# The FFN of the first two token blocks computed together, each prepared pair of weight tiles used for both

## The chip, the cores and the metric

One core of a Trainium2 chip runs the kernel. The metric is device time in microseconds (us) of one execution. Engines are named as in the profile: PE (TensorE; its weight loads are PEld), DVE (VectorE), ACT (ScalarE), POOL (GpSimd) and SP (SyncE, which issues nearly all DMAs here). L74 means line 74 of the kernel before, unless the text says that a line is of the changed kernel.

## The reference, cut to what matters

`x` has 4 sequences of 1024 tokens with 512 channels. After a layer norm `xn`, an attention branch and a gated FFN branch are added to `x`:

```
xn  = layernorm(x)
h   = rmsnorm(xn) * qkv_norm_w
q, k, v = h @ ternary(qkv_w).T              # 16 heads of 32
# chunks of 128 tokens, with a state S carried from chunk to chunk:
o   = scale * (decayed causal (q k^T) v  +  decayed q S);  S = lam_T * S + decayed k^T v
att = rmsnorm(rmsnorm(o, norm_w), proj_norm_w) @ ternary(proj_w).T
ffn = (silu(xn @ w_gate.T) * (xn @ w_up.T)) @ w_down.T     # hidden size 2048
out = x + att + ffn
```

`ternary(w)` rounds a matrix to -1, 0 or 1 times its mean magnitude.

## The kernel before, in words

**Number format.** PE works on fp16. An f32 value is kept as a pair of fp16 tiles, `hi` (rounded, after a scaling by a power of two) and `lo` (the rest). A product of two such pairs takes three matmuls (hi·hi, hi·lo, lo·hi).

**Tiling.** The 4096 tokens are 8 blocks of 512. `ffn_up` (L681) takes one block and one of 16 hidden tiles `j` of 128: 12 matmuls of 128x512 for the gate and 12 for the up product, each into a PSUM bank `psf` (three banks, shared with `ffn_down`). ACT takes the silu (L693), DVE multiplies (L696), ACT and POOL split the result into the pair `ghl` (L699, L700). `ffn_down` (L704) multiplies `ghl` with the down weights `wd`, and DVE adds the sums to `acc` (L720), which holds `x` and goes out when all its parts are in. A block's FFN is 48 steps; a step is what lies between two `yield`s.

**Weight preparation.** The FFN weights come in f32. Two hidden tiles (gate, up and down parts of each) are a group; there are 8. `load_group` loads the six tiles (256 KB each), `group_sums` finds their magnitudes on DVE (L312) and ACT (L316), `group_scale` makes a common power of two with a small PE matmul with a matrix of ones, a few small DVE operations behind it (L326 to L335), and `group_conv` makes hi (ACT L352) and lo (DVE L354, or POOL L357 and L360), and stores the gate and up pair to DRAM (`gu_d`, L362). Block 0 uses the tiles as they come out of this: `ffn0` (L743) walks over the 8 groups, with the down product of one group during the up products of the next, so that `acc` of block 0 gets 8 FFN sums per 128 tokens. `stage` (L777) places the preparation in the steps of block 0: `LEAD` says how many steps ahead of a group's use (six steps a group) each part of it is recorded. Blocks 1 to 7 run `ffn` (L730), which reads the prepared pairs back (512 KB per tile) and adds two sums per 128 tokens.

**Layer norm.** `ln_stats` computes the statistics on DVE (L389, L390), the inverse root on POOL (L395, L396) and normalises on DVE (L402). Block 0 is transposed into `xT` by PE (`ln0`, L412). Later blocks (`ln`, L430) get hi from ACT (L436), lo from POOL (L437) and are transposed by DMA (L438), during the last steps of the block before. One `xT` tile holds 512 tokens, and every up matmul reads all 512.

**Attention.** It runs in halves of 256 tokens (`att_half`, L458), whose steps are interleaved with those of the FFN. The list `at` (L841) gives the step at which each half begins: 36, then every 22.4 steps. A half computes q and k (L470 to L495; four pieces, ACT L479 and DVE L480 split them into hi and lo), writes them to DRAM (`sd`, L484) and reads them back head by head (`qst`, `kst`, L487), and k is also transposed by DMA (`kn`, L492). Then come v, the scores (one PSUM bank `pss`, DVE L545, ACT L547, POOL L548), the state and the projection. `prep` and `prep_proj` prepare the ternary weights beside block 0.

**Order.** A scheduler decides the order of the instructions on DVE, ACT, POOL and SP when the kernel is built; each engine then runs its list in order. PE keeps the program's order (L74).

Of the kernel before, what the change touches and what calls it, by code (L numbers as in the profile page):

```python
# [28 lines left out]
def block_kernel(ctx, tc, x, qkv_w, qkv_nwT, proj_w, proj_nwT, proj_nw, norm_w, s, w_gu, w_down, out):  # L29
# [83 lines left out]
    pnw_bc = ct([P, C], F32, "pnw_bc")  # L113
    ones = pnw_bc[:, :P]
    V.memset(ones, 1.0)
    nwT = ct([P, CC], F32, "nwT")
# [47 lines left out]

    HOLD = {"qst": (4, 1), "kst": (4, 1), "qhl": (2, 1), "khl": (2, 1)}

# [116 lines left out]
    def raw_pair(g, kind):  # L283

        if kind == 2:
            return [t32(), t32()]
        if g == 0 and kind == 0:
            t = wt([P, 2, C], F32, "kn", 1)
            return [t[:, 0, :], t[:, 1, :], t]
        return [wt([P, C], F32, *(("ghl", 8) if g % 2 else ("xin", 4) if g else ("xn2", 2))) for _ in range(2)]  # L290

# [120 lines left out]
    def ln0():  # L412

        rs, xts = lnst.pop(0)
        xT = wt([P, 2, CC, HB], F16, "xT", 1)
        blk[0] = [xT, None, rs]
        low = []
        for k in range(4):
            pt = bank(ps_f if k == 3 else ps_a, (P, CC, P))
            for c in range(CC):  # L420
                T.transpose(pt[:, c, :], xts[k][:, c * P : (c + 1) * P], ident)
            hi, lo = (xT[:, n, :, k * P : (k + 1) * P] for n in range(2))
            A.activation(hi, pt, AF.Copy, scale=XS)
            low.append((lo, pt, XS, hi, ALU.mult, ALU.subtract))
        for k in range(4):
            if k == 2:
                yield
            V.scalar_tensor_tensor(*low[k])

    def ln(b):  # L430
        rs, xts = lnst.pop(b)
        xT = wt([P, 2, CC, HB], F16, "xT", 1)
        blk[b] = [xT, None, rs]
        for k in range(4):
            xn2 = wt([P, 2 * C], F16, "xn2", 2).rearrange("p (a c) -> p a c", a=2)
            A.copy(xn2[:, 0, :], xts[k])  # L436
            G.tensor_tensor(xn2[:, 1, :], xts[k], xn2[:, 0, :], ALU.subtract)  # L437
            SY.dma_start_transpose(  # L438
                xT[:, :, :, k * P : (k + 1) * P].rearrange("p a c t -> p (a c) t"),
                xn2.rearrange("p a c -> p (a c)"),  # L440
            )
            yield
# [15 lines left out]
    def att_half(b, half):  # L458
# [5 lines left out]
        kst = wt([P, 4, CC, UT], F16, "kst", 1)  # L464
        qhl = wt([P, 2, CC, UT], F16, "qhl", 1)
        khl = wt([P, 2, CC, UT], F16, "khl", 1)
        qhi, qlo = qhl[:, 0], qhl[:, 1]
        khi, klo = khl[:, 0], khl[:, 1]
        kn = wt([P, 2, CC, 2, P], F16, "kn", 1)
        for i in range(4):  # L470
            dhi, dlo = (qhi, qlo) if i < 2 else (khi, klo)
            pair = slice(2 * (i % 2), 2 * (i % 2) + 2)
            pq = bank(ps_a, (P, 2, UT))
            for n in range(2):
                w = slice((2 * i + n) * P, (2 * i + n + 1) * P)
                for c in range(CC):
                    T.matmul(pq[:, n, :], wqkT[:, c, w], hhi[:, c, :], start=(c == 0), stop=False)
                    T.matmul(pq[:, n, :], wqkT[:, c, w], hlo[:, c, :], start=False, stop=(c == CC - 1))
            A.activation(dhi[:, pair, :], pq, AF.Copy, scale=QS)  # L479
            V.scalar_tensor_tensor(dlo[:, pair, :], pq, QS, dhi[:, pair, :], ALU.mult, ALU.subtract)  # L480
            if i % 2 == 1:
                src, dst, sel = (qhl, qst, (0, 1, 0)) if i == 1 else (khl, kst, (0, 0, 1))
                sd = dram.tile([P, 2 * CC * UT], F16, tag=f"sd{i}", name=nm("sd"), bufs=2)
                SY.dma_start(sd, src.rearrange("p a c t -> p (a c t)"))  # L484
                sv = sd.rearrange("(h d) f -> d h f", d=D)
                for g in range(3):
                    SY.dma_start(  # L487
                        dst[D * g : D * g + D].rearrange("p h c t -> p h (c t)"),
                        sv[:, :, sel[g] * CC * UT : (sel[g] + 1) * CC * UT],
                    )  # L490
                if i == 3:
                    SY.dma_start_transpose(  # L492
                        kn.rearrange("p a c k q -> p (a c k) q"), khl.rearrange("p a c t -> p (a c t)")
                    )
            yield  # L495

        vs, vrs = [], []
        for k in range(2):
# [3 lines left out]
            for c in range(CC):  # L502
                T.matmul(pv, hhi[:, c, hs], wvT[:, c, :], start=(c == 0), stop=False)
                T.matmul(pv, hlo[:, c, hs], wvT[:, c, :], start=False, stop=(c == CC - 1))
            vhl = wt([P, 2 * C], F16, "vhl", 5).rearrange("p (h a d) -> p h a d", a=2, d=D)
            pvh = pv.rearrange("p (h d) -> p h d", d=D)
# [21 lines left out]
        for k in range(2):  # L528
            u = Chunk()
            u.kn, u.vr = kn[:, :, :, k, :], vrs[k]  # L530
            u.g = g0 + k
# [43 lines left out]
        def state(u):  # L575
            pkv = bank(ps_a, (P, CC, P))
            for c in range(CC):
                ch = slice(c * P, (c + 1) * P)
                kh, kl = u.kn[:, 0, c, :], u.kn[:, 1, c, :]
                vh, vl = (v[:, ch] for v in u.vr)  # L580
# [16 lines left out]
        def norms(u):  # L597
# [19 lines left out]
            if u.g < B * N // P - 2:  # L617
                on = wt([P, 2 * C], F16, "vhl", 5).rearrange("p (a c) -> p a c", a=2)
                A.copy(on[:, 0, :], u.o3)  # L619
                G.tensor_tensor(on[:, 1, :], u.o3, on[:, 0, :], ALU.subtract)  # L620
                oT = wt([P, 2 * C], F16, "vhl", 5).rearrange("p (a c t) -> p a c t", a=2, t=P)
                SY.dma_start_transpose(
                    oT.rearrange("p a c t -> p (a c) t"), on.rearrange("p a c -> p (a c)")
                )
                u.oh, u.ol = oT[:, 0], oT[:, 1]
# [99 lines left out]
    def load_acc(b):  # L725
        for k in range(4):
            acc[4 * b + k] = load_x(4 * b + k, "acc", 8)
            parts[4 * b + k] = 1 + (2 if b else NG)

# [12 lines left out]

    def ffn0():  # L743
        prev = None

        def down(ks):
            g, gts = prev
            for k in ks:
                for _ in ffn_down(0, k, range(2 * g, 2 * g + 2), gts, icg[:, g : g + 1]):
                    pass  # L750

        for g in range(NG):
            nxt = g + 1 < NG
            gts = []
            for r in range(2):
                j = 2 * g + r
                for n, _ in enumerate(ffn_up(0, j, gu0.pop(j), bsc0, gts, G)):
                    stage(6 * g + 3 * r + n)
                    yield
                if g == 0 and r == 0:  # L760
                    load_acc(0)
                stage(6 * g + 3 * r + 2)
                if prev is not None and nxt:
                    down((2 * r, 2 * r + 1))
                    yield
            if not nxt:
                down((0, 1))
                yield
                down((2, 3))
                yield  # L770
            prev = (g, gts)
        down((0, 1))
        yield
        down((2, 3))
        yield

    def stage(i):  # L777
# [8 lines left out]
        for lead, f in zip(LEAD, (load_group, group_sums, group_scale, conv0, conv1)):  # L786
            g, m = divmod(i + lead, 6)
            if m == 0 and 0 < g < NG:
# [8 lines left out]

    LEAD = (16, 8, 5, 4, 2)
    load_group(0)
# [6 lines left out]
    with after(gate):  # L806
        group_conv(0, 1, (0, 1))
        group_sums(0, (2,))
        load_group(1)
        for i in range(5 - max(LEAD), 0):  # L810
            if i == -4:
                norm_sums()
            stage(i)

    def prep():
        qw = load_rows(qkv_w, ("qst", "kst", "qhl", "khl"))
        SY.dma_start(nw_bc, norm_w.partition_broadcast(P))
        yield from prep_qkv_w(qw)

    def prep_proj():  # L820
        pw = [wt([P, C], F32, "acc", 8) for _ in range(4)]
        for r in range(4):
            SY.dma_start(pw[r], proj_w[r * P : (r + 1) * P, :])
        yield
        with after(lg):
# [19 lines left out]
    halves = []  # L845
    side, side2 = prep(), prep_proj()
    t = 0
    for b in range(NB):
        lns = iter(())
        for i, _ in enumerate(ffn(b) if b else ffn0()):  # L850
            for _ in range(int(0.8 * t) - int(0.8 * (t - 1))):
                next(side, 1)
            if t == 12 or 28 <= t < 34 or 36 <= t < 56 and t % 2:
                next(side2, 1)
            if t in mh:
# [7 lines left out]
            t += 1  # L863
            if t == 6 * NG - 6:
                SY.dma_start(pnw_bc, proj_nw.partition_broadcast(P))
            if b + 1 < NB:
                if i == TS - (22 if b else 15):
                    ln_stats(b + 1)
                if i == TS - (9 if b else 5):
                    lns = ln(b + 1)  # L870
                if i in ((TS - 8, TS - 7, TS - 5, TS - 4) if b else range(TS - 4, TS)):
                    next(lns, 1)
        for _ in lns:
            pass
        if b == 0:
            half_scales(0)
# [53 lines left out]
```

## Time and profile before

| | us |
|---|---|
| median of 3 runs | 1369.12 (1367.17 to 1370.31) |
| the profiled execution: its own time | 1368.61 |
| its span in the trace | 1366.7 |
| PE busy | 1322.6 (97%), 8514 matmuls |
| DVE, ACT, POOL busy | 719.9, 550.3, 619.6 |
| chain that ended last: PE, DVE, POOL, issue, DMA | 79%, 7%, 7%, 3%, 3% |
| DMA | 178.11 MB, 130 GB/s in the mean, 343 GB/s in the first of 40 slices |

A matmul of 128x512 is listed with 0.38 us, but matmuls overlap: twelve of them in a row start 2.59 us before the next twelve. "Idle" below is time in which no PE row lies; each gap hides about 0.16 us more, the overlap that it interrupts. The granted TensorE clock is 1.00 or 0.50 at any moment; a mean between them says how long it was at half.

### The profile page before, as it was taken

The numbers are of one execution on the slowest core, as the hardware profiler recorded it, in microseconds if no ns is written. First come the engines' busy times: TensorE is split into PE (matmuls) and PEld (weight loads), VectorE is DVE, ScalarE is ACT, GpSimd is POOL, SyncE is SP. The second block draws the span as 40 slices with busy tenths as digits, with TensorE's granted clock in tenths as the row PEclk, the third lists the DMA queues.
The fourth block names the chain that finished last, engine by engine and source line by source line (L and its number), as shares of the span: only waits on it lengthen the run. The fifth ranks groups of instructions, "written<-read, shape, count | busy, mean of one in ns | idle before, by whom it ended". The sixth has DMA issues, their size and how long they took to land.

```text
span 1366.7 us, 21760 instructions
## 1 busy us (share of the span) xinstructions
PE 1322.6 (97%) x8514; PEld 695.6 (51%) x8514; DVE 719.9 (53%) x1415; ACT 550.3 (40%) x1033; POOL 619.6 (45%) x603
## 2 busy tenths in 40 slices
PE   5998989999999999999999999999999999999998
PEld 2443445554555545455455545555555555565554
DVE  7897764445544354453644446453553445356444
ACT  6754443343433334333334243342424334244341
POOL 3657672444624254353634246342545245255451
PEclk9999999999999999999999999999999999999999
DMA  9833836146261554426363354626283444535420
GB/s 343 294 124 114 231 101 180 48 137 156 87 191 31 165 128 125 140 59 173 94 155 108 103 141 104 178 69 162 80 181 95 116 116 106 142 109 124 105 66 31
DMA packets 155974, 178.11 MB, mean 130 GB/s; under 512 B 101600, under 2 KB 101600, under 8 KB 155872
## 3 DMA queue, kind: packets, MB, share of 16 engines
q1 hardware_dynamic: 155728, 176.73, 47.0%
q8 instruction: 66, 1.08, 0.3%
q14 instruction: 36, 0.29, 0.1%
q10 hardware_dynamic: 144, 0.01, 0.0%
HBM read 119.55 MB, written 33.55 MB: 112 GB/s over the span
## 4 chain that ended last, share of the span: by engine, by line
PE 79%; DVE 7%; POOL 7%; issue 3%; DMA 3%; ACT 1%; SPq 0%; POOLq 0%; ACTq 0%; DVEq 0%
PE psf L74 58%; PE psa L74 19%; PE pss L74 2%; DMA xin<-in_x_dram 2%; DMA xT<-xn 1%; POOL t L548 1%; DVE acc L720 1%; POOL xn L437 1%; DVE t L696 1%; DVE gs L312 1%; POOL rs L396 1%; POOL wd L360 1%; DVE t L239 0%; POOL ghl L700 0%; POOL gu L360 0%
## 5 line engine op out<-in xcount | busy, mean ns | idle before, releaser
L74 PE MATMUL psf<-xT,gu 128*128 128x512 f16 x3072 | 703.4, 381 | 10.6 <-POOL gu L360 5.5
L74 PEld LDWEIGHTS <-gu 128*128 128x128 f16 x3072 | 294.7, 98 | 338.0 <-issue 10.1
L74 PE MATMUL psf<-wd,ghl 128*128 128x512 f16 x1536 | 352.3, 380 | 2.7 <-ACT t L693 1.1
L74 PEld LDWEIGHTS <-ghl 128*128 128x128 f16 x1536 | 146.9, 98 | 164.3 <-issue 3.3
L548 POOL TENSOR_TENSOR t<-t,t 128x512 f16<-128x512 f32 x128 | 149.5, 1168 | 164.2 <-ACT t L547 163.9
L700 POOL TENSOR_TENSOR ghl<-t,ghl 128x512 f16<-128x512 f32 x86 | 102.6, 1193 | 163.4 <-ACT ghl L699 150.2
L696 DVE SCALAR_TENSOR_TENSOR t<-psf,bsc,t 128x512 f32<-128x512 f32 x128 | 95.9, 749 | 121.2 <-PE psf L74 104.8
L699 ACT CAST ghl<-t 128x512 f16<-128x512 f32 x128 | 79.0, 617 | 176.1 <-DVE t L696 175.6
L545 DVE SCALAR_TENSOR_TENSOR t<-pss,rs,mask 128x512 f32<-128x512 f32 x128 | 95.3, 744 | 77.2 <-PE pss L74 74.7
L693 ACT ACTIVATE t<-psf,ug 128x512 f32<-128x512 f32 x128 | 87.5, 684 | 98.0 <-PE psf L74 96.6
L74 PE MATMUL psa<-h,wqkT 128*128 128x256 f16 x1024 | 122.2, 273 | 0.0
L519 POOL TENSOR_TENSOR t<-t,t 128x512 f16<-128x512 f32 x28 | 32.6, 1163 | 195.3 <-ACT t L518 195.3
L547 ACT CAST t<-t 128x512 f16<-128x512 f32 x128 | 79.1, 618 | 101.9 <-DVE t L545 96.3
L74 PEld LDWEIGHTS <-wqkT 128*128 128x128 f16 x1024 | 99.7, 98 | 23.4
L720 DVE SCALAR_TENSOR_TENSOR acc<-psf,c,acc 128x512 f32<-128x512 f32 x56 | 41.8, 747 | 63.0 <-PE psf L74 62.7
L74 PEld LDWEIGHTS <-t 128*128 128x128 f16 x1040 | 47.6, 97 | 35.0 <-POOL t L548 3.4
L74 PE MATMUL psa<-wvT,h 128*128 128x512 f16 x256 | 60.5, 379 | 0.0
L74 PE MATMUL pss<-qst,kst 96*128 96x128 f16 x512 | 49.2, 218 | 8.7 <-DVE t L545 6.5
L74 PE MATMUL psa<-wpT,vhl 128*128 128x512 f16 x240 | 56.7, 379 | 0.0
L620 POOL TENSOR_TENSOR vhl<-t,vhl 128x512 f16<-128x512 f32 x30 | 34.7, 1155 | 48.0 <-ACT vhl L619 48.0
L573 POOL TENSOR_TENSOR t<-t,t 128x512 f32<-128x512 f32 x28 | 36.1, 1288 | 44.1 <-DVE t L572 18.6
L508 DVE SCALAR_TENSOR_TENSOR vhl<-psa,rs,vhl 128x512 f16<-128x512 f32 x32 | 24.0, 749 | 56.2 <-ACT vhl L507 54.5
(188 smaller groups left out, 1340.8 us busy)
## 6 DMA issues: line engine op xcount, KB each, us to landing
gu<-gu_d SPq DMA_DIRECT2D x112, 512.0 KB, 3.6
qst<-sd SPq DMA_DIRECT2D x48, 256.0 KB, 4.8
kst<-sd SPq DMA_DIRECT2D x48, 256.0 KB, 4.7
xin<-in_x_dram SPq DMA_DIRECT2D x32, 256.0 KB, 3.0
acc<-in_x_dram SPq DMA_DIRECT2D x32, 256.0 KB, 2.8
gu_d<-gu SPq DMA_DIRECT2D x16, 512.0 KB, 4.1
sd<-qhl SPq DMA_DIRECT2D x16, 512.0 KB, 2.6
sd<-khl SPq DMA_DIRECT2D x16, 512.0 KB, 3.3
```

Of the source, the lines that this page charges most:

```text
L74: tc.keep_in_program_order(nc.tensor.matmul(*a, **k))
L519: G.tensor_tensor(vrl, vr, vrh, ALU.subtract)
L545: V.scalar_tensor_tensor(sm, pss, u.rk, mask[:, 4 * qd : 4 * qd + 4, :], ALU.mult, ALU.mult)
L547: A.copy(u.smh, sm)
L548: G.tensor_tensor(u.sml, sm, u.smh, ALU.subtract)
L573: G.tensor_tensor(u.o, u.o, oc, ALU.add)
L620: G.tensor_tensor(on[:, 1, :], u.o3, on[:, 0, :], ALU.subtract)
L693: pa = A.activation(sl, pm, AF.Silu, scale=ug[:, j // 2 : j // 2 + 1])
L696: pv = V.scalar_tensor_tensor(gf, pm, bs[:, j // 2 : j // 2 + 1], sl, ALU.mult, ALU.mult)
L699: A.copy(ghl[:, 0, :], gf)
L700: E.tensor_tensor(ghl[:, 1, :], gf, ghl[:, 0, :], ALU.subtract)
L720: V.scalar_tensor_tensor(acc[g], ps, c, acc[g], ALU.mult, ALU.add)
```

## The change

The first two blocks are computed in one loop of 96 steps, `ffn01`, in place of `ffn0` and of `ffn(1)`. Each group is prepared once, at half the rate per step, and its two tiles serve block 0 and block 1; each block's `acc` gets the sum of every group, so block 1 also gets 8 FFN sums per 128 tokens and reads no prepared pair back. In the first group the order is both tiles for block 0, then both for block 1. Block 1's layer norm moves from the end of block 0 to the start of the kernel, and the attention halves keep their step numbers.

Other edits: `xT` has two buffers instead of one, `vhl` four instead of five; q and k go to DRAM in four pieces of 256 KB through a tile `qk` with three buffers, and k is transposed in two pieces as they come; the matrix of ones is a broadcast column; `proj_w` is loaded into the tile `qst` once the qkv weights are done with it, and its preparation follows theirs in one sequence.

```diff
-        xT = wt([P, 2, CC, HB], F16, "xT", 1)
+        xT = wt([P, 2, CC, HB], F16, "xT", 2)
...
         for i in range(4):
-            dhi, dlo = (qhi, qlo) if i < 2 else (khi, klo)
+            p = i % 2
+            hl = wt([P, 2, 2, UT], F16, "qk", 3)
...
-            if i % 2 == 1:
-                SY.dma_start(sd, src.rearrange("p a c t -> p (a c t)"))
...
+            SY.dma_start(sd[:, :, p], hl.rearrange("p a c t -> p a (c t)"))
+            if i > 1:
+                SY.dma_start_transpose(
+                    kn[:, p].rearrange("p a c k q -> p (a c k) q"), hl.rearrange("p a c t -> p (a c t)")
+                )
...
-            parts[4 * b + k] = 1 + (2 if b else NG)
+            parts[4 * b + k] = 1 + (2 if b > 1 else NG)
...
-    def ffn0():
+    def ffn01():
...
+        def down(units):
+            g, gts = prev
+            for u in units:
+                b, k = divmod(u, 4)
+                for _ in ffn_down(b, k, range(2 * g, 2 * g + 2), gts[b], icg[:, g : g + 1]):
+                    pass
         for g in range(NG):
             nxt = g + 1 < NG
-            gts = []
-            for r in range(2):
-                j = 2 * g + r
-                for n, _ in enumerate(ffn_up(0, j, gu0.pop(j), bsc0, gts, G)):
-                    stage(6 * g + 3 * r + n)
+            gts = [], []
+            order = [(0, 0), (1, 0), (0, 1), (1, 1)] if g else [(0, 0), (0, 1), (1, 0), (1, 1)]
+            for m, (b, r) in enumerate(order):
+                for n, _ in enumerate(ffn_up(b, 2 * g + r, gu0[2 * g + r], bsc0, gts[b], G)):
+                    stage(12 * g + 3 * m + n)
                     yield
...
                 if prev is not None and nxt:
-                    down((2 * r, 2 * r + 1))
+                    down((2 * m, 2 * m + 1))
                     yield
...
-            g, m = divmod(i + lead, 6)
+            g, m = divmod(i + lead, 12)
...
-    LEAD = (16, 8, 5, 4, 2)
+    LEAD = (14, 10, 8, 7, 4)
...
     with after(gate):
         group_conv(0, 1, (0, 1))
         group_sums(0, (2,))
+        ln_stats(1, 1)
+        for _ in ln(1):
+            pass
         load_group(1)
-        for i in range(5 - max(LEAD), 0):
-            if i == -4:
-                norm_sums()
-            stage(i)
+        norm_sums()
...
-    for b in range(NB):
+    for b in range(1, NB):
         lns = iter(())
-        for i, _ in enumerate(ffn(b) if b else ffn0()):
+        n_steps = TS if b > 1 else 2 * TS
+        for i, _ in enumerate(ffn(b) if b > 1 else ffn01()):
```

## The prediction

> **What bounds the kernel now.** I read the engine totals and the slices of the page first, then the busy time by stretches, then PE's waits and its timeline where a stretch shows idle time.
>
> ```profile
> PE 1322.6 (97%) x8514; PEld 695.6 (51%) x8514; DVE 719.9 (53%) x1415; ACT 550.3 (40%) x1033; POOL 619.6 (45%) x603
> DMA  9833836146261554426363354626283444535420
> ```
>
> PE is busy 97% of the span, and the change leaves its matmuls as many and as large as they are. So the change can only move PE's idle time and the time at half clock. Busy time by stretches (columns: stretch, its length, PE, PEld, DVE, ACT, POOL busy, clock, DMA share, GB/s) says where those are:
>
> ```profile
> 0.00:34.00 34.00, 18.88 (x71) 9.46 (x72) 26.66 (x77) 22.04 (x49) 12.38 (x26) 0.95 0.94 343
> 34.00:100.00 66.00, 64.21 (x306) 30.02 (x305) 59.61 (x137) 44.11 (x94) 38.74 (x30) 1.00 0.61 209
> 100.00:131.00 31.00, 24.61 (x108) 10.80 (x107) 21.41 (x39) 15.80 (x33) 26.33 (x21) 0.89 0.36 122
> 131.00:177.00 46.00, 41.46 (x238) 22.02 (x237) 33.93 (x62) 19.55 (x34) 30.77 (x29) 1.00 0.75 201
> 177.00:335.00 158.00, 155.86 (x1023) 82.64 (x1021) 80.89 (x152) 61.22 (x111) 68.90 (x69) 1.00 0.48 130
> 335.00:515.00 180.00, 174.74 (x1175) 92.36 (x1174) 84.92 (x166) 65.05 (x121) 80.95 (x84) 1.00 0.42 115
> ```
>
> Idle in the five from 34 on: 1.8, 6.4, 4.5, 2.1, 5.3. The rows that own it, from PE's waits between 90 and 200 and from PE's timeline at the head and at 117 (start, length, what, idle before):
>
> ```profile
> PE psf L74 <- POOL gu L360: 5.5, 2, 5.0
> PE pss L74 <- DMA kst<-sd: 1.8, 1, 1.8
> PE psf L74 <- DMA xT<-xn: 1.2, 1, 1.2
> ...
> 26.68 0.87 PE L74 MATMUL psa<-gm,pnw_bc 128*128 128x3 f32 x4 [2.84 <-DVE gm L318]
> 27.41 9.30 PE L74 MATMUL psf<-xT,gu 128*128 128x512 f16 x36
> ...
> 125.26 4.26 PE L74 MATMUL psf<-xT,gu 128*128 128x512 f16 x10 [5.03 <-POOL gu L360]
> ```
>
> At 120 PE waits 5.03 us for POOL to finish a weight tile, then runs ten matmuls in 4.26 us where ten take 2.32: a wait of that size costs 1.9 us more at half clock. The 2.84 us wait at the head does the same (36 matmuls in 9.30, where they take 7.93).
>
> **What the change can take away.** Block 0's preparation, now in 48 steps beside the start of the attention, is spread over 96. In each group PE gets 31 us of FFN instead of 15.6, while POOL's four L360 and two L357 (4 x 1.2 + 2 x 1.7 = 8.2 us) stay the same. So the 5.03 us wait and its half clock should go. The wait for block 1's `xT` at 177 goes too, because its layer norm is no longer there. Waits of that kind and the bursts around them, 34 to 335: idle 1.8 + 6.4 + 4.5 + 2.1 = 14.8, half clock 1.9, and about twelve gaps that each hide 0.16 of overlap, 1.9. Sum 18.6 us.
>
> What stays of it? DVE gets 24 more adds (L720 at 0.747: 17.9 us) and the second half of the preparation while attention runs. I put it near 17 of 25 us from 43 to 344, twelve stretches of 25. The quiet stretch above (DVE 12.8 of 25) loses 2.1 in 158, which makes 4 over 300. Six stretches of the trace with DVE at 16 or more of 25 (at 75, 125, 500, 675, 825, 1225) lose 0.1, 0.3, 2.5, 2.2, 0.0 and 1.3, mean 1.07, which makes 12.8. The ones that lose little are those without a layer norm next to the scores, as this stretch will be, so I take 5 and keep 4 to 12.8. Gain 13.6.
>
> **What it costs at the head.** The built program's order of instructions shows that block 1's layer norm has to be finished before PE's fifth up product, the first for block 1. Rows for its price, from the groups kept apart by form, and from the DMA issues:
>
> ```profile
> L437 POOL TENSOR_TENSOR xn<-xin,xn 128x512 f16<-128x512 f32 x8 | 10.1, 1267 | 8.3 <-ACT xn L436 8.3
> L389 DVE BATCH_NORM_STATS2 st<-xin 128x6 f32<-128x512 f32 x16 | 11.0, 690 | 20.3 <-DMA xin<-in_x_dram 20.2
> L402 DVE TENSOR_SCALAR xin<-xin,mv,rs 128x512 f32<-128x512 f32 x15 | 10.1, 716 | 2.4 <-POOL rs L400 2.2
> ...
> xT<-xn SPq DMA_TRANSPOSE x28, 3.5
> kn<-khl SPq DMA_TRANSPOSE x16, 6.4
> ...
> nw_bc<-in_norm_w_dram SPq DMA_DIRECT2D x1, 256.0 KB, 11.5
> ```
>
> First matmul: two reductions of group 1 (L312, 0.675 each) and a small operation now stand on DVE ahead of group 0's scale, 1.5 us. A third stands ahead of its first lo part, 0.7. So 24 matmuls that ended at 23.7 end at 25.9. The wait that follows shrinks: before it was for group 1's sums, now only for the magnitude of group 0's down part, which DVE has at about 26.3. With 0.7 for the small matmul, PE goes on at 27.0 without half clock, and 24 more end at 32.2. Before they ended at 27.41 + 1.37 + 5.18 = 34.0.
>
> Then block 1's `xT`. From group 0's scale (17.2) to the last normalised tile DVE has 38 instructions: four lo parts 3.0, four reductions 2.7, four statistics 2.8, four aggregates 0.7, four normalisations 2.9, one L696 0.75, and some twenty small ones 3.0; sum 15.9, end 33.1. From 32.3 POOL still has a small product, three lo parts, one `ghl` and another small one: 0.3 + 3 x 1.27 + 1.26 + 0.4 = 5.8, end 38.1. Each transpose waits for its lo part, the last lands 3.5 later, at 41.6. PE idles 9.4 and then loses 1.9 at half clock: it is at its 49th up matmul 43.5 - 34.0 = 9.5 us later than before. Behind the transposes SP holds group 2's loads and two `gu_d` writes; group 2 is used 24 steps on, some 60 us, so they are covered. The wait also lets DVE, ACT and POOL catch up.
>
> [...] The trace has 1.27 (POOL L437) beside 0.75 to 0.88 on DVE (L354), so 1.4 to 1.7 times. [...] The sum goes by the row.
>
> **The rest.** No gu reads for block 1: 16 of 512 KB less, no PE wait names them, 0. The q and k pieces: 48 more SP issues of about 0.4 us, but k's transpose (L492, 3.3 to 4.8 us of SP) no longer stands whole before the kst reads; kst was waited for 1.8 us in all, counted above. Bounds for later blocks: from -5.3 (all idle of 335 to 515) to +1.8 (one such wait more); I take 0, since PE's order there is unchanged. Four `vhl` buffers: no wait for one shows; 0, upper bound one wait like the 2.84 with its 1.4. Ones as a broadcast and the later `proj_w`: 0: the matmuls with ones are a dozen of 0.2 to 0.4, and the preparation of `proj_w` is recorded up to about step 33, while `qst` is first overwritten near step 38 and the projection comes near 58; if it were late, the row for a wait on `qst` is 0.4.
>
> **Sum.** -18.6 + 5 + 9.5 = -4.1 against the profiled execution's own 1368.6 (span 1366.7, 1.9 around it): 1364.5. It lies 0.5 under the median of the runs, so 1365.0. About 0.2%, 2.7 us, is what a measurement here can tell from no change.
>
> **The rivals.**
> *Transposes held up (slower).* The place is the head: the first 50 us of the trace run DMA full (share 0.94), and transfers issued at 24 to 26 there took 11.5 us. If the last transpose takes that in place of 3.5, PE waits 8 longer: 1373. It decides from a landing of about 10.3 us on (3.5 and 4.1 + 2.7 more). Against: some 11.5 MB stand before the transposes, at 343 GB/s or more done by about 35, before the last is issued.
> *DVE limits the attention.* What stays is 12.8 in place of 5: 1372.8. For: 24 adds and the preparation fall beside scores that have one PSUM bank. Against: at 75 DVE is busy 24.75 of 25 and PE idles 0.1.
> *Later blocks gain.* kst earlier removes the idle of 335 to 515: 1359.7. For: the SP time of L492. Against: only 1.8 us of waits name kst.
>
> **How the numbers follow.** Forecast 0.47 (own range 1362 to 1370: DVE's rows start up to a tenth closer than their lengths, 1.6 less, and 0.9 less stays; upward 9 stays and POOL is 1 later); transposes 0.20; DVE 0.20; later blocks 0.13. Faster: 0.37 of the forecast and 0.13; same: 0.10, 0.02 of the transposes and 0.06 of DVE; slower: 0.18 and 0.14. Range: the third rival with the forecast's low end, 1357, to the first with 9 staying, 1377.
>
> **What would show it.** Right: a PE wait of 7 to 11 us for `xT` near 32 to 42, half clock behind it, no PE wait for POOL L360, under 8 us idle from 43 to 335. Wrong: no wait at the head or one over 15, PE waiting at `pss` for DVE all through the first 340 us, or idle that moves by more than 5 after 340.

## The result, and the profile after

| | kernel before | changed kernel |
|---|---|---|
| median, us | 1369.26 (1367.17 to 1370.31) | 1399.98 (1398.97 to 1401.95) |
| ratio | | 1.0228 (95% interval 1.0210 to 1.0246) |
| span of the profiled execution | 1366.7 | 1397.2 |

The change makes the kernel 2.3% slower, 30.5 us by the spans; the forecast was 4.1 us faster. From here on, line numbers of the changed kernel are some lines lower: L691 (was L696) multiplies silu and up product, L694 (was L699) makes the `hi` part of `ghl`, L403 (was L402) normalises, L438 and L439 (were L437 and L438) make a token tile's `lo` part and transpose it, L543 (was L548) makes the scores' `lo` part, L611 (was L616) ends the attention's norms, L715 (was L720) adds a sum to `acc`.

Engine totals of the page after, then the DMA slices:

```profile
PE 1329.7 (95%) x8514; PEld 697.5 (50%) x8514; DVE 734.2 (53%) x1433; ACT 549.4 (39%) x1033; POOL 625.8 (45%) x618
DMA  9332625237571562517454354624364353436430
```

The matmuls are as many as before. PE's busy time rose by 7.1, most of it by matmuls at half clock (PE was busy for 22.3 us at half clock, before for 10.8), and the other 23.4 of the 30.5 is new idle time. DVE has 14.3 more to do, by 18 instructions more in all. None of these sums says where it was lost. Busy time by stretches, with bounds shifted so that they hold about the same work as those of before (columns: stretch, length, PE, PEld, DVE, ACT, POOL, clock, DMA share, GB/s):

```profile
0.00:47.00 47.00, 22.24 (x81) 10.76 (x82) 34.56 (x88) 24.84 (x53) 27.22 (x49) 0.85 0.94 319
...
110.00:138.00 28.00, 25.51 (x123) 11.88 (x121) 20.04 (x39) 12.94 (x26) 16.21 (x13) 1.00 0.29 94
138.00:178.00 40.00, 40.00 (x244) 21.85 (x242) 23.33 (x41) 20.17 (x39) 20.55 (x17) 1.00 0.57 145
178.00:363.00 185.00, 170.80 (x1081) 88.79 (x1079) 118.21 (x232) 83.28 (x158) 109.61 (x107) 0.96 0.46 116
363.00:545.00 182.00, 177.15 (x1182) 93.40 (x1181) 85.66 (x173) 66.55 (x124) 78.15 (x78) 1.00 0.47 125
...
900.00:950.00 50.00, 42.94 (x315) 21.72 (x314) 23.21 (x45) 18.05 (x34) 27.13 (x29) 0.93 0.22 65
```

From 110 to 178, where the kernel before idled 6.4 and 4.5, PE now idles 2.5 and 0. From 178 to 363 it idles 14.2, with the clock at 0.96, where 158 us of the kernel before lost 2.1. And a stretch of 50 us in the sixth block (block 5), which the change was not meant to touch, idles 7.1. PE's waits name the places (what is waited for, us in total, times, longest):

```profile
PE psf L74 <- DMA xT<-vhl: 11.5, 1, 11.5
PE psa L78 <- DVE xin L403: 8.9, 3, 8.1
PE psf L74 <- ACT ghl L694: 7.1, 1, 7.1
PE psf L74 <- DVE acc L715: 6.2, 4, 3.1
PE psf L74 <- DVE t L691: 6.1, 3, 2.3
PE psa L74 <- POOL t L543: 5.2, 3, 2.7
```

The wait for POOL L360 that the change was to remove is gone. In its place stand the head's wait for block 1's `xT` (foreseen, 9.4), one wait of 7.1 for `ghl`, and waits for sums, silu products and scores of 2 to 3 each. (The wait of 8.1 for L403 is the kernel's start, and the kernel before has 8.2 there.)

To add this up I follow PE through each trace and note when it has done the same amount of matmul work (each matmul counted with its time in an uninterrupted row, 0.2155 us for 128x512; from start to start the traces have 0.215 or 0.216). The table says how many us later than in the kernel before that point is reached. It is used for the experiments too; their edits follow below.

| matmul work done, us | what ends about there | after | e3 | e5 | e6 | e9 | e12 | e13 | e14 |
|---|---|---|---|---|---|---|---|---|---|
| 20 | the head | 10.8 | 11.0 | -0.8 | 10.1 | 3.3 | 4.5 | -1.1 | 4.2 |
| 100 | before's 5.03 us stall | 5.8 | -0.3 | -0.5 | 5.2 | -0.8 | -0.3 | -0.9 | -0.8 |
| 140 | block 0 of before | 0.7 | -5.5 | 9.5 | 0.5 | -5.6 | -5.5 | 1.7 | -5.6 |
| 310 | block 1 | 19.9 | 0.1 | 11.8 | 14.4 | 8.9 | 3.3 | 1.5 | -1.0 |
| 850 | | 22.0 | 1.4 | 15.3 | 13.6 | 9.1 | 5.0 | 1.5 | -0.6 |
| 900 | middle of block 5 | 30.5 | 10.5 | 23.5 | 13.6 | 9.1 | 5.0 | 1.6 | -1.6 |
| 1290 | the end | 30.5 | 10.5 | 23.5 | 13.6 | 9.1 | 5.0 | 1.5 | -0.6 |

So the changed kernel loses 10.8 at the head, gains 10.1 up to 140, loses 19.2 up to the end of block 1, and 8.5 more at one place in block 5. The last is the plainest to read. From the timelines of the changed kernel there (start, length, engine, line, what, idle before):

```profile
926.31 2.87 DVE L403 TENSOR_SCALAR xin<-xin,mv,rs 128x512 f32<-128x512 f32 x4 [0.25 <-POOL rs L401]
...
930.05 1.15 POOL L438 TENSOR_TENSOR xn<-xin,xn 128x512 f16<-128x512 f32 x1
931.16 1.26 POOL L597 TENSOR_TENSOR t<-t,nw_bc 128x512 f32<-128x512 f32 x1
932.39 1.15 POOL L438 TENSOR_TENSOR xn<-xin,xn 128x512 f16<-128x512 f32 x1
...
933.93 0.57 POOL L604 TENSOR_TENSOR f<-f,mhalf 128x1 f32<-128x1 f32 x1
...
937.83 0.75 DVE L611 SCALAR_TENSOR_TENSOR t<-t,f,pnw_bc 128x512 f32<-128x512 f32 x1
938.62 0.75 DVE L691 SCALAR_TENSOR_TENSOR t<-psf,bsc,t 128x512 f32<-128x512 f32 x1
...
940.07 5.72 PE L74 MATMUL psf<-wd,ghl 128*128 128x512 f16 x15 [7.06 <-ACT ghl L694]
```

A layer norm (L403, L438) stands between the steps of the attention's norms (L597 to L611). Each of those steps crosses from DVE to POOL and back, and L691, whose data has been ready since PE's last up product, stands behind the last of them in DVE's order. PE then waits 7.06 and runs 15 matmuls in 5.72 where fifteen take 3.4. In the kernel before, the same stretch of the attention has no layer norm in it; its last four normalisations come 98 us further on, when a block ends:

```profile
908.98 0.75 DVE L616 SCALAR_TENSOR_TENSOR t<-t,f,pnw_bc 128x512 f32<-128x512 f32 x1
909.65 0.75 DVE L696 SCALAR_TENSOR_TENSOR t<-psf,bsc,t 128x512 f32<-128x512 f32 x1
...
1007.30 1.92 DVE L402 TENSOR_SCALAR xin<-xin,mv,rs 128x512 f32<-128x512 f32 x4 [1.59 <-POOL rs L400]
```

Both are the layer norm of the last block, since each trace has one such group for each block. What moved it half a block ahead is the question of e5, e6 and e13.

### The profile page after: what moved, and what is told of

The parts are those of the page before. It is cut to its first block, busy times and chain, and to the rows that moved or that the text cites. A ratio compares the mean times of both kernels' runs of the same rounds, so it can differ in the third digit from the quotient of the medians.

```text
span 1397.2 us, 21825 instructions
## 1 busy us (share of the span) xinstructions
PE 1329.7 (95%) x8514; PEld 697.5 (50%) x8514; DVE 734.2 (53%) x1433; ACT 549.4 (39%) x1033; POOL 625.8 (45%) x618
## 4 chain that ended last, share of the span: by engine, by line
PE 77%; DVE 8%; POOL 6%; DMA 5%; issue 3%; ACT 1%; SPq 1%; POOLq 0%; DVEq 0%; ACTq 0%
PE psf L74 57%; PE psa L74 18%; PE pss L74 2%; DMA xin<-in_x_dram 2%; DMA xT<-xn 1%; DMA xin<-in_w_gu_dram 1%; DVE acc L715 1%; POOL xn L438 1%; POOL t L543 1%; POOL rs L397 1%; DVE st L390 1%; DVE t L691 1%; POOL xin L358 1%; DVE t L540 1%; DMA vhl<-vhl 0%
## 5 line engine op out<-in xcount | busy, mean ns | idle before, releaser
L74 PE MATMUL psf<-xT,gu 128*128 128x512 f16 x3072 | 704.8, 381 | 24.8 <-DMA xT<-vhl 11.5
L74 PE MATMUL psf<-wd,ghl 128*128 128x512 f16 x1536 | 358.3, 384 | 11.4 <-ACT ghl L694 7.1
L543 POOL TENSOR_TENSOR t<-t,t 128x512 f16<-128x512 f32 x128 | 149.0, 1165 | 156.3 <-ACT t L542 156.1
L695 POOL TENSOR_TENSOR ghl<-t,ghl 128x512 f16<-128x512 f32 x92 | 108.6, 1181 | 217.8 <-ACT ghl L694 198.8
L691 DVE SCALAR_TENSOR_TENSOR t<-psf,bsc,t 128x512 f32<-128x512 f32 x128 | 95.8, 749 | 132.4 <-PE psf L74 118.2
L694 ACT CAST ghl<-t 128x512 f16<-128x512 f32 x128 | 79.0, 617 | 177.6 <-DVE t L691 176.8
L477 DVE SCALAR_TENSOR_TENSOR qk<-psa,qk 128x512 f16<-128x512 f32 x64 | 44.2, 691 | 112.5 <-ACT qk L476 107.4
L476 ACT ACTIVATE qk<-psa 128x512 f16<-128x512 f32 x64 | 38.1, 595 | 79.4 <-PE psa L74 78.2
L715 DVE SCALAR_TENSOR_TENSOR acc<-psf,c,acc 128x512 f32<-128x512 f32 x48 | 35.9, 749 | 58.1 <-PE psf L74 57.9
L615 POOL TENSOR_TENSOR vhl<-t,vhl 128x512 f16<-128x512 f32 x30 | 34.6, 1154 | 49.4 <-ACT vhl L614 49.4
```

Source lines behind the costliest of these rows:

```text
L74: tc.keep_in_program_order(nc.tensor.matmul(*a, **k))
L476: A.activation(hl[:, 0], pq, AF.Copy, scale=QS)
L477: V.scalar_tensor_tensor(hl[:, 1], pq, QS, hl[:, 0], ALU.mult, ALU.subtract)
L543: G.tensor_tensor(u.sml, sm, u.smh, ALU.subtract)
L691: pv = V.scalar_tensor_tensor(gf, pm, bs[:, j // 2 : j // 2 + 1], sl, ALU.mult, ALU.mult)
L694: A.copy(ghl[:, 0, :], gf)
```

## The experiments

**e1 to e4: the head, POOL, the preparation, the sums.** Theories at the start: the preparation, spread over steps that hold attention, gets in front of the attention's and the FFN's own work on DVE, ACT and POOL; rivals were the head alone, POOL's share of the `lo` parts, and the 24 added sums. e1 transposes block 1's tokens by PE, as block 0's: `ln1` has 16 PE transposes, and ACT makes `hi` and DVE `lo`:

```diff
-        for _ in ln(1):
-            pass
...
+                if g == 0 and m == 2:
+                    ln1()
```

> The changed kernel, but block 1's normalised tokens are transposed by PE (16 small matmuls, placed after the first four up products), with ACT and DVE writing the pair, instead of ACT copy, POOL subtraction and DMA transpose. Theory (the head costs 10.8 us because block 1's layer norm ends late: 11.5 us wait and half clock): DVE's last normalisation ends near 33, then 4 transposes, one ACT and one DVE step per tile instead of 10 us of POOL and DMA; the wait falls to 2 to 4 us and the time by 6 to 9 us, to 1391 to 1394. Rival (the start is bound by weight loads, so whatever is later takes over): PE then waits for group 1 or for down weights and the time falls by less than 3 us.

Measured: 1399.29 (1398.35 to 1400.52). The wait of 11.5 is split into waits of 5.0 and 1.7, and PE is 6.0 late at the head in place of 10.8, but that counts the 16 transposes, 3.4 of PE's time, as work done. Without them it is 10.2 late at the head, 14.9 in place of 19.9 at the end of block 1, and about level with the changed kernel in the middle (21.7 and 22.0 at 600 us of work). A miss: a shorter wait here is not worth its size.

e2 makes every `lo` part of a weight tile by one DVE operation in place of two of POOL, or ACT and POOL:

```diff
-            if kind == 0 or g == 0 and kind == 1 or g <= 1 and kind == 2:
+            if kind < 3:
                 lv = V.scalar_tensor_tensor(lo, src, w1, hi, ALU.mult, ALU.subtract)
```

> The changed kernel, but every lo part of a prepared weight tile is one DVE operation (0.75 us), so that POOL loses its two scalings (1.7 to 2.0) and four subtractions (1.15) per group and ACT two scalings. Theory (between 140 and 340 us PE waits because weight preparation stands in front of attention work on POOL: waits for POOL L543 at 190 and 282, and because raw tiles are freed late, so the next group's loads are late): these waits go, 6 to 10 us less, 1390 to 1394. Rival (DVE is what limits these blocks, with its 24 more adds): 3 to 4.5 us of DVE more per group make it slower, 1402 to 1412.

Measured: 1396.87 (1394.62 to 1397.27). The waits for POOL L543 at 190 and 282 are gone (5.2 us in all became 1.0), but a wait of 3.36 for a silu came at 285. Less than expected.

e3 prepares only groups 0 and 1 and uses their tiles for all others; loads, sums, scales, conversions and stores of six groups are left out, and the matmuls stay as many and as large:

```diff
-            if m == 0 and 0 < g < NG:
+            if m == 0 and 0 < g < 2:
...
-                for n, _ in enumerate(ffn_up(b, 2 * g + r, gu0[2 * g + r], bsc0, gts[b], G)):
+                for n, _ in enumerate(ffn_up(b, (2 * g + r) % 4, gu0[(2 * g + r) % 4], bsc0, gts[b], G)):
```

> The changed kernel without the preparation of groups 2 to 7: the first two groups' tiles are used in their place, so the loads, sums, scales, conversions and stores of six groups are left out. It bounds what preparation costs after the head. If the 30 us that PE loses between 43 and 340 come from preparation beside the attention: PE loses under 8 there and the time is 1372 to 1380. If they come from the 24 additional sums of block 1 on DVE: PE still loses 20 or more there, 1392 to 1400. The wait of 7 us at 933 is in a block that neither touches; if it is an accident of the scheduled order it may go or stay.

Measured: 1378.85 (1378.63 to 1381.37), the theory's number. No gap of over 0.5 us is left between 43 and 315, and PE is where it was in the kernel before at the end of block 1 (0.1 in the table). So preparing six groups costs 20 us: 6.1 before the attention begins (at 138 in the changed kernel, the row at 100) and 13.7 beside it. How much of this is the work itself and how much its loads stays open. The changed kernel holds the f32 gate and up tiles of groups 2 to 7 in `xin` alone, where the kernel before put every second group into `ghl`, and ACT waits 16.6 us in all for f32 weight tiles to land, before 5.4; no run has that edit by itself. Even so, 10.5 of loss is left at the end, though the head is made up for by the end of block 1: 9.1 of it is lost at the wait in block 5, still 7.1 long.

e4 leaves out 24 of block 1's 32 sums:

```diff
-        if len(js) % 4:
+        if len(js) % 4 and (b != 1 or js[0] % 8 == 6):
             add_acc(b * 4 + k, pd, c)
```

> The changed kernel without 24 of block 1's 32 FFN sums (PE's matmuls stay, the sums of groups 0, 1, 2, 4, 5 and 6 of block 1 are left out): DVE has 17.9 us less, as many sums as before. If the additional sums are what makes PE wait between 43 and 340: 10 to 20 us less, 1380 to 1390. If preparation beside attention does: less than 5 us, 1395 to 1402.

Measured: 1393.93 (1391.2 to 1397.44), between the two expectations. The 17.9 us of sums cost about 6, a third of their length; the runs of e4 spread over 6.2, so this is rough.

**e5, e6, e13: who moved the layer norm.** It is in all of e1 to e4. The order of the built programs pointed to the second `xT` buffer. e5 is the kernel before with two of the change's other edits (q and k in pieces, `vhl` with four buffers) and two `xT` buffers, e13 the same with one; e6 is the changed kernel with one for blocks 1 to 7:

```diff
     def ln0():
-        xT = wt([P, 2, CC, HB], F16, "xT", 2)
+        xT = wt([P, 2, CC, HB], F16, "xT0", 1)
...
     def ln(b):
-        xT = wt([P, 2, CC, HB], F16, "xT", 2)
+        xT = wt([P, 2, CC, HB], F16, "xT", 1)
```

> The kernel before, with the change's other edits and none of the joint loop: q and k through pieces in `qk`, k transposed in two pieces, `vhl` with four buffers, and `xT` with two buffers. The order of the instructions shows that with the second `xT` buffer block 6's layer norm moves ahead of the norms of block 5's first half on POOL and DVE, as in the changed kernel; without it (pieces and `vhl` alone) it stays where it was. Theory (second buffer): a PE wait of about 7 us for `ghl` near 910 with half clock behind it, 1375 to 1379 in all, if the pieces are worth nothing. Rival (the wait comes from the joint loop): no such wait, 1366 to 1371.

> The changed kernel, but block 0's `xT` is a tile of its own and blocks 1 to 7 share one buffer as before. Theory (second buffer): the wait of 7.2 us in block 5 and its half clock go, 8 to 9 us; at the end of each block a wait of about 1 us for `xT` can come back, of block 1 perhaps more: 1391 to 1396. Rival (the wait comes from the joint loop): 1398 to 1402.

> The kernel of e5 with `xT` back at one buffer: the kernel before with q and k in pieces, k's two transposes and `vhl` with four buffers. Theory (all of e5's 24 us came from the second `xT` buffer): no wait over 6 us after 130, 1365 to 1371. Rival (the pieces or the four `vhl` buffers cost part of it): 1375 to 1390.

Measured: e5 1392.12 (1390.26 to 1394.6), e13 1369.16 (1367.17 to 1370.06), ratio 1.0006 (0.9996 to 1.0015); e6 1381.59 (1380.77 to 1384.62), ratio 1.0094 (1.0077 to 1.0111). The pieces and `vhl` together are worth nothing either way. **The second `xT` buffer alone costs the kernel before 23 us, and its removal gives the changed kernel 18.** Both are more than I had expected, and for e5 the table says why: besides the 8.2 in block 5, e5 loses 10.0 from 100 to 140, where e13 loses 2.6. (The norm that moves in block 5 is the eighth of eight, so block 7's, and not block 6's as the expectation has it.) The lines of e5 from 160 on, SP, DVE, ACT and PE:

```profile
160.26 1.26 SPq L438 DMA_TRANSPOSE xT<-xn  x1
161.57 0.58 SPq L162 DMA_DIRECT2D acc<-in_x_dram  x1
162.20 0.91 SPq L162 DMA_DIRECT2D xin<-in_x_dram  x2
...
165.58 0.69 DVE L389 BATCH_NORM_STATS2 st<-xin 128x6 f32<-128x512 f32 x1 [7.09 <-DMA xin<-in_x_dram]
166.19 0.73 DVE L502 SCALAR_TENSOR_TENSOR vhl<-psa,rs,vhl 128x512 f16<-128x512 f32 x1
166.84 0.74 DVE L508 SCALAR_TENSOR_TENSOR t<-psa,rs,lsm 128x512 f32<-128x512 f32 x1
...
167.62 0.62 ACT L512 CAST t<-t 128x512 f16<-128x512 f32 x1 [5.25 <-DVE t L508]
168.14 0.68 ACT L687 ACTIVATE t<-psf,ug 128x512 f32<-128x512 f32 x1
...
168.87 2.72 PE L74 MATMUL psf<-wd,ghl 128*128 128x512 f16 x6 [7.28 <-ACT t L687]
```

Read it from the bottom: PE waits 7.28 for a silu, the silu stands behind L512 on ACT, that waits for L508 on DVE, which stands behind L389, which waits 7.09 for the tokens of block 2. Their buffers came free only as block 1's tokens were made into `hi` and `lo`, which waited for the transposes of the first of them, and SP had a transpose and a load in front of their load. No engine is full: DVE stands idle for 7.09 with work behind the instruction that waits. With one buffer the layer norms are held back until the up products of a block have done with `xT`, a quiet place here; with two they may go as soon as anything is free, and the order written when the kernel is built puts them among the attention's steps. e6 has its last normalisations back at the end of a block, and the stretch in block 5 whole again (timeline, then busy time by stretches, as above):

```profile
1021.00 1.91 DVE L403 TENSOR_SCALAR xin<-xin,mv,rs 128x512 f32<-128x512 f32 x4 [1.59 <-POOL rs L401]
```

```profile
900.00:950.00 50.00, 49.29 (x363) 27.05 (x362) 23.71 (x52) 17.11 (x33) 19.46 (x19) 1.00 0.31 85
```

**e7: bursts or load.** One of the six tiles of a group is converted per step, in place of three in one step, twice (`LEAD` now has the load, the sums, the scale and the six tiles):

```diff
-    LEAD = (14, 10, 8, 7, 4)
+    LEAD = (14, 10, 8, 7, 6, 5, 4, 3, 2)
```

> The changed kernel with the conversions of a group spread: one of the six tiles a step (7 to 2 steps ahead of the group) in place of three tiles in one step, twice (7 and 4 ahead). The work is the same. Theory of bursts (several conversions in a row stand in front of the scores and silus on ACT and POOL): the waits at 190, 247 and 282 shrink, 1386 to 1394. Theory of load (DVE, ACT and POOL have too much to do beside the attention wherever it is put): 1396 to 1402.

Measured: 1400.81 (1399.17 to 1401.84). The waits for the scores' `lo` part on POOL at 192.8 and 284 are as long as in the changed kernel (2.66 and 2.17), and the one for a product at 340 grew from 2.25 to 3.04. The theory of bursts falls in this form: recording the work in smaller portions does not keep it from standing in front of the attention.

**e8 and e10: the attention later, and the statistics later.**

```diff
-    at = [round(36 + 22.4 * n) for n in range(2 * NB - 2)]
+    at = [round(56 + 21 * n) for n in range(2 * NB - 2)]
```

> The changed kernel with the attention begun at step 56 and then every 21 steps, in place of 36 and every 22.4 (its last halves end about where they did). Theory (preparation beside attention costs the 20 us that leaving it out gave back): two groups more are prepared with no attention beside them, about 40% of 20 us less, but the later halves stand closer by 6%: 1388 to 1396. Rival (the cost lies in the preparation's own pace against the FFN, wherever the attention is, or the closer halves give it back): 1397 to 1406.

e10 adds to e8:

```diff
-                if i == n_steps - (22 if b > 1 else 14):
+                if i == n_steps - 12:
                     ln_stats(b + 1)
```

> The kernel of e8 (attention from step 56 every 21, two `xT` buffers) with each later block's statistics recorded 12 steps before the end of the block before in place of 22 (14 for block 2). Theory (with two buffers the layer norm drifts ahead into the scores and norms, wherever they stand): the 7 us that e8 loses after 380 shrink by 3 to 6: 1376 to 1379. Rival (the losses there are those of the closer halves): 1381 to 1385.

Measured: e8 1382.11 (1380.0 to 1382.28), better than the theory asked for. At the end of block 1 e8 is 5.1 behind the kernel before in place of 19.9, a gain of 14.8 where the theory had 8, and near the 13.7 that e3 gained beside the attention. Another 8.5 is a reason the theory did not have: the wait in block 5 is absent, since the attention's norms now fall elsewhere against the layer norm. Some 6 are lost again after block 1, to the closer halves or to layer norms among them; no run parts the two. e10, 1381.09 (1379.68 to 1382.78), changes nothing that can be told, and its normalisations start within 1.4 us of those of e8: where the statistics are recorded does not place them, so it tests neither of its theories.

**e9, e12, e11, e14, e15: is the joint loop itself worth something?** e9 is e6 with block 0's down products of group 0 moved into the head's wait:

```diff
+                if g == 0 and m == 1:
+                    prev = (0, gts)
+                    down(range(4))
+                    prev = None
...
-                    down((2 * m, 2 * m + 1))
+                    if g > 1 or m > 1:
+                        down((2 * m, 2 * m + 1))
                     yield
```

> The kernel of e6 (blocks 1 to 7 share one `xT` buffer), and block 0's four down products of group 0 come right after block 0's up products of that group, that is in PE's wait for block 1's `xT`, in place of between the products of group 1. No work is added. Theory (the head's wait is a latency that other matmuls can fill): 24 matmuls, 5.2 us, go into the wait of 12.1, and the half clock behind it may go: 1374 to 1377 against the 1381.6 of e6. Rival (the down part's conversion and the `acc` loads are themselves not ready then, or hold up block 1's tokens on DVE): 1379 to 1384.

> The kernel of e9 with all lo parts of the weight tiles as one DVE operation, as in e2, whose waits for POOL L543 (5.8 us in e6) go: 1371 to 1374 if e9 is at 1376. If DVE's 12 to 20 us more give it back in waits for the silu and the sums: no better than e9 or up to 3 us worse.

Measured: e9 1376.74 (1375.41 to 1377.86), 4.9 less than e6. PE's rows at the head of e9 show why not 5.2 and the half clock besides: the filling waits itself, for the `lo` part of the down tile on DVE, between block 1's tokens.

```profile
34.32 0.59 PE L74 MATMUL psf<-wd,ghl 128*128 128x512 f16 x2 [2.77 <-DVE wd L355]
36.30 1.03 PE L74 MATMUL psf<-wd,ghl 128*128 128x512 f16 x2 [1.38 <-ACT ghl L694]
```

e12, e9 with the `lo` parts on DVE: 1372.08 (1371.94 to 1373.65), 4.7 less. e11 takes e9's head and starts the attention at step 48 (48, 68, 88, 109, then from 129 on every 22), with an `xT` of its own for block 1 only; e14 is e11 with the `lo` parts on DVE, and e15 is e14 from step 54 (54, 73, 92, 110, 129):

```diff
-    at = [round(36 + 22.4 * n) for n in range(2 * NB - 2)]
+    at = [round(48 + 20.25 * n) for n in range(4)] + [round(129 + 22 * n) for n in range(2 * NB - 6)]
```

> The kernel of e9 with the attention begun at step 48, four halves 20 steps apart, and back on the first schedule from the fifth half on (129, then every 22); block 1 has an `xT` of its own and all other blocks share one, as the later make-h of block 1 needs. If the gains of e6, e8 and e9 add up, with e8's halved: 1366 to 1371. If the later start and the single buffer mend the same waits: 1374 to 1378.

> The kernel of e11 with all lo parts on DVE, as in e12. If the waits that e11 has for POOL L543 (5.9 us) go as they did from e9 to e12: 1366 to 1369, about the time of the kernel before or a little below. If DVE, fuller by it, gives them back in waits for its sums: 1370 to 1374.

> The kernel of e14 with the attention begun at step 54 and its first halves 19 steps apart, in place of 48 and 20. If the start past the preparation is what counts: 1364 to 1367. If the closer halves cost as much as they save: 1367 to 1371.

Measured: e11 1371.63 (1369.68 to 1373.68), e14 1367.10 (1365.9 to 1367.96), ratio to the kernel before 0.9990 (0.9982 to 0.9999), e15 1373.79 (1369.95 to 1375.16). e11 lies just above what was expected if the gains add, e14 met its first expectation, and e15 is worse than both of its own. Its runs spread over 5.2 us, more than those of any kernel here but e4, and why they do stays open. PE's waits of e14:

```profile
PE psa L78 <- DVE xin L404: 8.8, 3, 8.0
PE psf L74 <- DVE t L692: 5.3, 3, 2.1
PE pss L74 <- DVE t L541: 4.0, 4, 1.8
PE psf L74 <- DVE acc L716: 3.2, 2, 2.7
```

So four repairs, none of them touching the joint loop's idea, take back all of the 30.5 by the spans: one `xT` buffer 16.9 (1397.2 to 1380.3), the filled head 4.5 (1375.8), `lo` parts on DVE 4.1 (1371.7), the attention at 48 with block 1's own `xT` 5.6 (1366.1). What is left of the joint loop's gain is 0.1%, with an interval that ends just under 1. In the column of e14 PE is 5.6 ahead at 140 and 1.0 ahead at 310. Part of that lead is only work put off: at 140 e14 has made 36 of the 48 `hi` parts of the weights and has begun its attention 31 us later, while the kernel before has made all 48. From there to 310 PE waits 3.2 for sums and 2.1 for a product.

## Why the prediction was wrong, by its own steps

**The head: right in size, in part by luck.** It said that block 1's `xT` would be ready at 41.6, PE waiting 9.4 with half clock behind it, 9.5 late in all. The matmuls went on at 42.79 after a wait of 11.51, twelve of them in 4.78, and PE was 10.8 late. Two errors nearly cancel in this. POOL's last `lo` part of block 1 ended at 36.02, not at 38.1. But the last transpose was issued only at 38.96, because SP spends 1.23 to 3.08 us on each of the four and has a weight load between them, and it landed some 3.6 later. The rival of transposes held up, which needed a landing of 10.3, did not occur: the slowest took 6.6. From the timeline of the changed kernel:

```profile
42.79 4.78 PE L74 MATMUL psf<-xT,gu 128*128 128x512 f16 x12 [11.51 <-DMA xT<-vhl]
```

**The stall and the `xT` wait that go: right.** From 20 to 140 the changed kernel makes up 10.1, and PE never waits for POOL's part of a weight tile (L361, was L360).

**"What stays of it", 5 with 4 to 12.8: mis-sized.** The sum allowed a net gain of 13.6 from 34 to 335. With the buffer's part taken out (e6), PE goes from 10.1 late at 20 to 14.4 late at 310, a loss of 4.3, so what stays is 18 more than the term, about 23. The step that failed is its rows. I took stretches in which DVE was as full as it would be and read their idle time, and so priced how busy an engine is. DVE was about as full as I put it (16.2 of 25 us from 43 to 344, for 17), and PE still idled 14.4 from 43 to 335, where under 8 was to show that I was right. Nor was the stretch without a layer norm, as the choice of 5 assumed: block 2's stands at 298 to 302. The loss here is one of order: a preparation step on ACT, DVE or POOL stands in front of a silu, a product or a score, and it waits for a load or for another engine. ACT and DVE of the changed kernel at 245 show it: ACT waits 4.42 for a weight tile to sum, the v of the attention stands behind it, DVE waits 7.09 for that v, and PE waits 3.09 for the sum behind it in DVE's list.

```profile
245.47 0.63 ACT L317 ACTIVATE junk<-xin 128x512 f16<-128x512 f32 x1 [4.42 <-DMA xin<-in_w_gu_dram]
...
248.69 0.75 DVE L503 SCALAR_TENSOR_TENSOR vhl<-psa,rs,vhl 128x512 f16<-128x512 f32 x1 [7.09 <-ACT vhl L502]
249.36 0.74 DVE L509 SCALAR_TENSOR_TENSOR t<-psa,rs,lsm 128x512 f32<-128x512 f32 x1
250.02 1.40 DVE L715 SCALAR_TENSOR_TENSOR acc<-psf,icg,acc 128x512 f32<-128x512 f32 x2
...
250.81 4.42 PE L74 MATMUL psf<-xT,gu 128*128 128x512 f16 x12 [3.09 <-DVE acc L715]
```

e3 prices the preparation at 20 us, 13.7 of it beside the attention, e4 the sums at 6 (they overlap), e12 POOL's and ACT's part in the `lo` parts at 4.7. That the order is what costs is read from such chains in the trace; no run changes the order alone. The rival of DVE limiting the attention does not describe it either: PE waits at `pss` for DVE 5.2 us in the changed kernel and 6.5 in the one before.

**The second `xT` buffer: not priced at all.** It was named in the change and left out of the sum, since more buffers seemed only to relax a wait. It is the largest of the four repairs: 16.9 of 30.5 by the spans of e6, and by itself it costs the kernel before 23 (e5 against e13).

**"The rest: I take 0, since PE's order there is unchanged": wrong**, with 10.6 lost after 310 against a bound of +1.8. PE's order was unchanged, but the order on DVE and POOL, which the built program shows as plainly, was not. The bound came from the idle of blocks in which the layer norm stood at a block's end. With one `xT` buffer (e6) PE makes up 0.8 after 310, so this loss is the buffer's too. The misses add up: the 34.6 between the forecast and the result are 16.9 for the buffer, 17.9 for what stays, 0.6 at the head, less this 0.8.

**The pieces of q and k and the four `vhl` buffers at 0: right** (e13, 1.0006). The rival that had them gain falls with it.

**POOL's speed.** The prediction put POOL at 1.4 to 1.7 times the time of DVE. In the changed kernel the same subtraction (L695) took 1.16 us on POOL and 0.69 on DVE in the median, 1.7 times. At the head this made no difference that the sum needed. Later it bears: in the median POOL took 1.92 for L358 and 1.15 for L361 where one DVE operation of 0.74 does both, and e12 and e14 gain 4.7 and 4.5 by leaving that to DVE, with PE's waits for the scores' L543, which stood behind it, down from 5.8 in e9 to 1.6 in e12.

## What to carry to other kernels

Where engines run fixed lists, a second buffer need not be a free relaxation: it can take away a wait that also kept work in its place, so compare the lists of every engine with and without it, and look for cross-engine chains that a new neighbour now splits. Price added work beside a pipeline by what stands behind each of its instructions and what that instruction waits for, not by how busy the engine becomes. When a change bundles several edits, run each side edit alone on the old kernel first; here e5 alone showed 23 us, and taking the second buffer out gave back 17 of the 30.5.

## What the runs showed of the hardware

In these runs the length of a gap did not by itself decide whether the half clock followed. In e9 a wait of 2.85 was followed by twelve matmuls in 2.75, full speed, in e14 a wait of 1.85 by 24 in 7.03, and in e6 one of 1.79 by 24 in 5.34, full speed again:

```profile
78.72 2.75 PE L74 MATMUL psf<-xT,gu 128*128 128x512 f16 x12 [2.85 <-DVE acc L715]
```

```profile
108.67 7.03 PE L74 MATMUL psf<-xT,gu 128*128 128x512 f16 x24 [1.85 <-DVE t L692]
```

```profile
116.28 5.34 PE L74 MATMUL psf<-xT,gu 128*128 128x512 f16 x24 [1.79 <-DVE t L691]
```

The 24 matmuls of e14 took 1.7 longer than those of e6 (7.03 less 5.34), and the mean clock of e14 from 110 to 138 was 0.95. What decides whether the half clock follows is not shown here.
